# A transformer block's down projection in 2x2 blocks with seven products for eight, in two groups of inner rows

## The chip, the cores and the metric

The kernel runs on one core of a Trainium2 chip. A core has a matrix engine (PE, with a separate row PEld for loading the stationary operand), a vector engine (DVE), a scalar engine (ACT), a general engine (POOL), a sync engine (SP) that here only issues transfers, and 16 DMA engines. Each engine runs its own instructions in order; waits between engines go through semaphores. The metric is the device time of one execution in microseconds (us); the figure for a kernel is the median of its runs.

## The reference

One block of a transformer on `x` of shape (2, 1024, 1024): modulated layer norm, attention with 32 heads, a residual, a second modulated layer norm and a gated feed-forward network whose weights are -1, 0 or +1. What the change touches is the last line of the network:

```python
gate = jnp.einsum('bsh,ih->bsi', x, Wg) * ag
up = jnp.einsum('bsh,ih->bsi', x, Wu) * au
h = jax.nn.silu(gate) * up
out = jnp.einsum('bsi,hi->bsh', h, Wd) * ad      # "down": INTER = 2752 inner rows, 1024 columns
...
x = x + gb * ffn(h2)
```

`gb * ad` is one row vector for each batch, made early and kept in DRAM as `gate_dram[5]`.

## The kernel before

All of it is float32. A product is made from `float32r` operands: the activations are split into a rounded part `hi` and a rest `lo = a - hi`, and both go through PE, while the ternary weights are exact. Counts (`ternary`, `exact`) check on the way that the weights are ternary and the split is exact; if a count is off, `general_block` computes everything again at the end. It doesn't run with these inputs.

The program has an attention stage (until about 1335 us), the output projection and the preparation of the second norm, gate and up for batch 0 and batch 1 (`gate_up`), and down. A list scheduler puts the instructions of each engine in an order. Matmuls are kept in program order in batch 1 of `gate_up` and in down (`pinned`).

Gate and up already use seven products for eight (`SEVEN`, lines 768 to 772): a block product of 2x2 blocks is made as seven products of sums of blocks. Bank `x` or `y` collects a product, some products are kept (`part`) and added to later ones (`MATE`), and four of them finish a quadrant (`QUAD`). `gate_up(b)` runs over eleven pairs `p` of inner blocks (10 of 2x128 rows, the last of 2x96). For each pair:

- `stage(p)` loads four weight tiles of 512 KB on SP's queue into two buffers, one for each half `kh` of the inner dimension. The pool `wst` has two buffers in all.
- `weight_operands` makes seven operands from them: `A11`, `A12`, `A22` are casts on ACT (lines 1611, 1612, 1617), and `S1`, `S2`, `S3`, `S4` are sums on POOL (lines 1613 to 1616). `S3` is the last reader of half 0.
- In batch 1 (and once at the end of batch 0) a tile `wdst` of 1 MB of the down weights goes through the same two buffers: it takes the buffer that `S3` has freed, is loaded on SP (line 1640), counted by DVE (`ternary`, lines 1570 and 1573) and written out to `wd_dram` on SP (line 1642). Half 1 of the next `stage` takes the buffer after it.
- PE runs 7 x 2 x 8 matmuls (gate and up). ACT copies the kept products out of the banks (line 1661), DVE adds, ACT applies silu, DVE multiplies, and SP writes the quadrant to `act_dram` (line 1684).

Down, before: eight token blocks of 128 rows in each of two batches. For each, ACT loads the block of `act_dram` (2816 values a partition) and casts it to `hi` (line 1722), DVE makes `lo` (line 1723), and PE runs 22 inner blocks x 2 halves of the columns x 2 parts = 88 matmuls of 128x512 into two banks (`dn`). DVE multiplies each bank by `gb` (line 1742), POOL adds the residual `x1` (line 1743), and SP writes the output. All of the down weights (11 MB) stand in SBUF, in buffers that `gate_up`'s token tiles leave one after another; their loads start while the last pair still runs.

Of the kernel before, what the change touches and what calls it, by code (L numbers as in the profile page):

```python
# [12 lines left out]
FP = mybir.dt.float32  # L13
FR = mybir.dt.float32r
# [5 lines left out]
P = 128  # L20
# [460 lines left out]
def kernel(  # L481
# [19 lines left out]
    nc = tc.nc  # L501
# [60 lines left out]


    hop2_dram = [dram.tile([P, 7, KC // 2, NJ, P], FP, tag=f"hs_{b}", name=f"hs_{b}") for b in range(B)]
    wd_dram = [dram.tile([P, 2, D], FP, tag=f"wd_{p}", name=f"wd_{p}") for p in range(NPR)]
    act_dram = [dram.tile([P, NJ, 2, NIC, P], FP, tag=f"act_{b}", name=f"act_{b}") for b in range(B)]

    ident = const.tile([P, P], FP, name="ident")
# [1017 lines left out]
    if True:  # L1586
# [6 lines left out]
            return ffp[i // 4].tile([P, 512], FP, tag=f"ff{i}", name=nm)  # L1593

        jkp = ff.enter_context(tc.tile_pool(name="junk", bufs=1))

        with gu:
            W_ORDER = ("A11", "A12", "S2", "S1", "S3", "S4", "A22")
# [27 lines left out]
            def gate_up(b):  # L1626
# [5 lines left out]
                for p in range(NPR):  # L1632
# [4 lines left out]
                    for p_ in down_checks[b].get(p, ()):  # L1637
                        r0, n = PAIRS[p_]
                        t = stp.tile([P, 2, D], FP, tag="wst", name=f"wdst_{p_}")
                        nc.sync.dma_start(t[0:n], wd_t[ds(r0, 2 * n), :].rearrange("(m p) e -> p m e", p=n))  # L1640
                        ternary(t[0:n].rearrange("p m e -> p (m e)"), 2 * NPR + p_, jkp)
                        nc.sync.dma_start(wd_dram[p_][0:n], t[0:n])
                    n = PAIRS[p][1]
                    if p + 1 < NPR or b + 1 < B:
                        st.append(stage((p + 1) % NPR))
# [2 lines left out]
                    for e, (c_, qa, qb_, q) in enumerate(SEVEN):  # L1648
                        done = {}
                        for i, mat in enumerate("gu"):  # L1650
                            ps = bank[mat, c_]
                            for k in range(KC // 2):
                                for hl in range(2):
                                    matmul(
                                        ps[0:n], W[qa][:, i, k, 0:n], tiles[e][:, hl, k, :],
                                        start=(q in ("P1", "P2", "P5") and k == 0 and hl == 0),
                                        stop=(k == KC // 2 - 1 and hl == 1), skip_group_check=True,
                                    )
                            if q in ("P1", "U2", "P5"):
                                part[mat, q] = ptp.tile([P, 512], FP, tag=f"{mat}{q}", name=f"{mat}{q}_{b}_{p}")  # L1660
                                nc.scalar.copy(part[mat, q][0:n], ps[0:n])
                            elif q == "U6":
                                done[mat] = ps
                            else:
                                t = part[mat, MATE[q]]
                                last_read[0] = nc.vector.tensor_add(t[0:n], t[0:n], ps[0:n])  # L1666
                                done[mat] = t
                        if q in QUAD:
                            m, h = QUAD[q]
                            ib = 2 * p + m  # L1670
                            g, u = done["g"], done["u"]
                            if q == "U6":
                                g, u = (
                                    ptp.tile([P, 512], FP, tag=f"{mat}{q}", name=f"{mat}{q}_{b}_{p}") for mat in "gu"
                                )
                            nc.scalar.activation(
                                g[0:n], done["g"][0:n], AF.Silu, scale=vt[0:n, R_AG + ib : R_AG + ib + 1]
                            )
                            ins = nc.vector.scalar_tensor_tensor(
                                u[0:n], done["u"][0:n], vt[0:n, R_AU + ib : R_AU + ib + 1], g[0:n], ALU.mult, ALU.mult  # L1680
                            )
                            if q == "U6":
                                last_read[0] = ins
                            nc.sync.dma_start(
                                act_dram[b][0:n, :, h, ib, :], u[0:n].rearrange("p (j t) -> p j t", j=NJ)
                            )
            for b in range(B):
                pinned[0] = b > 0
                gate_up(b)
            pinned[0] = True  # L1690

        with ExitStack() as dn:
            aip = [own(dn, f"ain{i}") for i in range(2)]
            lop0, hip0, hip1, lop1, gbp = (own(dn, n) for n in ("alo0", "ahi0", "ahi1", "alo1", "gb"))
            wdp = [own(dn, f"wd{p}") for p in range(NPR)]
            xp1, yp = own(dn, "x1in", 2), own(dn, "yout", 2)
            hip, lop = (hip0, hip1), (lop0, lop1)
            dlp = jkp
            wd = [wdp[p].tile([P, 2, D], FR, tag=f"wd{p}", name=f"wd_{p}") for p in range(NPR)]
            gb = []  # L1700

            def more_wd(which):
                for p in which:
                    n = PAIRS[p][1]
                    (nc.scalar if 0 < p < 8 else nc.sync).dma_start(wd[p][0:n].bitcast(FP), wd_dram[p][0:n])

            n1 = PAIRS[-1][1]
            for b in range(B):
                for j in range(NJ):
                    for h in range(2):  # L1710
                        t = 2 * j + h
                        a = aip[h].tile([P, NIC, P], FP, tag=f"ain{h}", name=f"a_{b}_{t}")
                        nc.scalar.dma_start(a[:, 0:WHOLE], act_dram[b][:, j, h, 0:WHOLE])
                        nc.scalar.dma_start(a[0:n1, WHOLE:NIC], act_dram[b][0:n1, j, h, WHOLE:NIC])
                        hi = hip[h].tile([P, NIC, P], FR, tag="ahi", name=f"hi_{b}_{t}")
                        lo = lop[h].tile([P, NIC, P], FR, tag="alo", name=f"lo_{b}_{t}")
                        cuts = [0, 4, 10, WHOLE] if (b, t) == (0, 0) else [0, WHOLE]
                        for v in (
                            *((slice(0, P), slice(u, w)) for u, w in zip(cuts, cuts[1:])),
                            (slice(0, n1), slice(WHOLE, NIC)),  # L1720
                        ):
                            nc.scalar.copy(hi[v[0], v[1]], a[v[0], v[1]])  # L1722
                            nc.vector.tensor_sub(lo[v[0], v[1]], a[v[0], v[1]], hi[v[0], v[1]].bitcast(FP))  # L1723
                        if (b, t) == (0, 0):
                            more_wd(range(NPR))
                            for b_ in range(B):
                                gb.append(gbp.tile([P, D], FP, name=f"gb{b_}"))
                                nc.scalar.dma_start(gb[b_], gate_dram[5][b_].partition_broadcast(P))
                        pss = [ffbank(f"dn_{b}_{t}_{n}") for n in range(2)]
                        for ib in range(NIC):  # L1730
                            rows = PAIRS[ib // 2][1]
                            for s_, src_ in enumerate((hi, lo)):
                                for n in range(2):
                                    matmul(
                                        pss[n], src_[0:rows, ib, :], wd[ib // 2][0:rows, ib % 2, ts(n, HALF)],
                                        start=(ib == 0 and s_ == 0), stop=(ib == NIC - 1 and s_ == 1),
                                    )
                        x1 = xp1.tile([P, D], FP, tag="x1", name=f"x1_{b}_{t}")
                        nc.sync.dma_start(x1, x1_dram[b * NT + t])
                        y = yp.tile([P, D], FP, tag="y", name=f"y_{b}_{t}")  # L1740
                        for n in range(2):
                            nc.vector.tensor_mul(y[:, ts(n, HALF)], pss[n], gb[b][:, ts(n, HALF)])  # L1742
                            nc.gpsimd.tensor_add(y[:, ts(n, HALF)], y[:, ts(n, HALF)], x1[:, ts(n, HALF)])  # L1743
                            nc.sync.dma_start(out[b, ts(t, P), ts(n, HALF)], y[:, ts(n, HALF)])
                        if (b, t) == (0, 0):
                            for i, src_ in enumerate((hi, lo)):
                                exact(
                                    src_[:, 0:4].rearrange("p k t -> p (k t)"), NCOUNT + i, ffbank(f"probe{2 + i}"), dlp
                                )
                        if (b, t) == (1, 2):  # L1750
                            verdict(dlp, ffbank)


    ff.close()
# [50 lines left out]
```

## Time and profile before

| | us |
|---|---|
| median of three runs (2352.24 to 2357.76) | 2355.83 |
| the profiled execution's own time | 2356.1 |
| its span on the core | 2354.4 |
| batch 0 to batch 1 of `gate_up` at PE | 1721 |
| first matmul of down | 2019.4 |
| last matmul of down starts | 2345.5 |

Busy time by engine and the main stages' shares, from the page's first part and from a table by stretches of time (columns: the stretch, then busy us and instructions of PE, PEld, DVE, ACT and POOL, then PE's granted clock, the DMA engines' busy share, GB/s):

```profile
PE 2198.6 (93%) x9713; PEld 1211.6 (51%) x9713; DVE 1266.9 (54%) x1820; ACT 841.8 (36%) x1701; POOL 886.8 (38%) x679
1800.00:2000.00 200.00, 196.71 (x861) 160.29 (x861) 103.25 (x106) 70.19 (x102) 76.92 (x32) 1.00 0.60 191
2100.00:2200.00 100.00, 100.00 (x442) 82.61 (x441) 27.62 (x20) 13.23 (x10) 12.69 (x10) 1.00 0.35 124
```

A busy share near 1 on PE in the last two lines says that matmuls follow each other almost without a gap there. The engines beside it are busy for about half of batch 1's gate and up and for about a fifth of down.

### The profile page before, as it was taken

Reading aid. Unit: us, or ns where it says so; the run is one execution under the profiler, and the core shown is the slowest. Engines: PE = TensorE matmul, PEld = TensorE weight load, DVE = VectorE, ACT = ScalarE, POOL = GpSimd, SP = SyncE. Lnnn points to the kernel's source line nnn. Section 1 sums busy time; section 2 is a strip of 40 time slices with the busy share of each in tenths; the row PEclk is TensorE's granted clock in tenths of the full one; section 3 lists DMA queues with packets and bytes.
Section 4 is the critical chain, followed back from the end, with each engine's and each line's share of the span. In section 5 each row is a group of like instructions: output and inputs, shape, how many; then the busy total and the mean of one; then the engine's idle time right before and its main releaser. Section 6 shows DMA issues by size and latency. Waiting matters only on the chain.

```text
span 2354.4 us, 26878 instructions
## 1 busy us (share of the span) xinstructions
PE 2198.6 (93%) x9713; PEld 1211.6 (51%) x9713; DVE 1266.9 (54%) x1820; ACT 841.8 (36%) x1701; POOL 886.8 (38%) x679
## 2 busy tenths in 40 slices
PE   6999999999999998798888797999989999999998
PEld 2444443333333332232222245888767788788887
DVE  5775752456556343366765566667785454322221
ACT  1322224444444445465555224333343333211110
POOL 2330202442336455666575653344343342011111
PEclk9999999999999999999999998999999999999999
DMA  9887777346246323754532466433476656833331
GB/s 368 307 305 274 287 269 242 133 135 221 94 155 217 134 90 141 209 166 130 153 117 90 127 201 219 128 114 117 131 267 214 201 182 198 334 126 126 124 104 38
DMA packets 264034, 423.18 MB, mean 180 GB/s; under 512 B 12940, under 2 KB 198604, under 8 KB 250132
## 3 DMA queue, kind: packets, MB, share of 16 engines
q1 hardware_dynamic: 256048, 382.00, 48.7%
q10 hardware_dynamic: 7844, 39.37, 4.6%
q8 instruction: 79, 1.29, 0.2%
q14 instruction: 63, 0.52, 0.1%
HBM read 290.51 MB, written 130.81 MB: 179 GB/s over the span
## 4 chain that ended last, share of the span: by engine, by line
PE 30%; DVE 7%; issue 7%; DMA 4%; POOL 3%; ACT 1%; SPq 0%; DVEq 0%; POOLq 0%; ACTq 0%
PE dn L742 12%; PE ux L742 4%; PE gx L742 4%; PE uy L742 4%; PE gy L742 3%; PE bank L742 2%; DVE junk L1570 2%; DVE p L1106 1%; DMA wst<-in_L_ffn_Wu_dram 1%; DMA wd<-wd 1%; DVE junk L1573 1%; PE sc L742 1%; DMA traw<-hs 1%; ACT p L1074 1%; PE av L742 1%
## 5 line engine op out<-in xcount | busy, mean ns | idle before, releaser
L1074 ACT ACTIVATE p<-sc,kw 128x128 f32<-128x128 f32 (+3 forms) x1024 | 422.6, 514 | 394.7 <-PE sc L742 374.9
L742 PE MATMUL bank<-wT,a 128*128 128x512 f32 x768 | 365.8, 610 | 14.5 <-ACT P L966 8.0
L1106 POOL TENSOR_TENSOR p<-p,p 128x1024 f32<-128x1024 f32 (+3 forms) x128 | 263.6, 2060 | 238.9 <-PE av L742 209.2
L1106 DVE TENSOR_TENSOR p<-p,p 128x1024 f32<-128x1024 f32 (+3 forms) x192 | 235.9, 1243 | 141.7 <-POOL p L1078 75.5
L742 PE MATMUL bank<-wB,a 128*128 128x512 f32 x576 | 270.3, 605 | 1.9 <-DVE raw L973 1.4
L742 PEld LDWEIGHTS bank<-wT,a 128*128 128x128 f32 x768 | 136.7, 191 | 199.0 <-issue 166.5
L742 PE MATMUL dn<-wd,hi 128*128 128x512 f32 (+1 forms) x704 | 218.4, 391 | 2.5 <-DMA wd<-wd 2.5
L742 PE MATMUL sc<-cq,ck 32*128 32x512 f32 (+3 forms) x1536 | 185.2, 543 | 37.5 <-ACT p L1074 28.7
L742 PE MATMUL dn<-wd,lo 128*128 128x512 f32 (+1 forms) x704 | 218.0, 391 | 1.0 <-DVE lo L1723 1.0
L1078 POOL TENSOR_SCALAR_AFFINE_SELECT p<-p 128x256 f32<-128x256 f32 x256 | 130.5, 522 | 187.0 <-ACT p L1074 177.5
L742 PE MATMUL av<-p,cv 128*32 128x512 f32 (+3 forms) x1536 | 169.9, 507 | 13.9 <-POOL p L1078 13.9
L742 PEld LDWEIGHTS bank<-wB,a 128*128 128x128 f32 x576 | 102.1, 189 | 145.8 <-issue 125.1
L1613 POOL TENSOR_TENSOR wS<-wst,wst 128x1024 fp32r<-128x1024 f32 (+1 forms) x22 | 53.5, 2430 | 304.2 <-DMA wst<-in_L_ffn_Wu_dram 213.9
L1743 POOL TENSOR_TENSOR y<-y,x 128x512 f32<-128x512 f32 x32 | 40.8, 1293 | 316.1 <-DVE y L1742 316.1
L742 PEld LDWEIGHTS dn<-wd,hi 128*128 128x128 f32 (+1 forms) x704 | 132.6, 189 | 30.9 <-DMA wd<-wd 3.0
L742 PEld LDWEIGHTS sc<-cq,ck 32*128 32x128 f32 x1536 | 62.8, 185 | 166.0 <-issue 97.9
L742 PEld LDWEIGHTS dn<-wd,lo 128*128 128x128 f32 (+1 forms) x704 | 132.6, 188 | 29.7 <-DVE lo L1723 1.5
L1742 DVE TENSOR_TENSOR y<-dn,gb 128x512 f32<-128x512 f32 x32 | 20.6, 686 | 209.0 <-issue 196.6
L1722 ACT CAST hi<-a 96x256 fp32r<-96x256 f32 (+4 forms) x34 | 42.5, 1300 | 247.3 <-PE dn L742 223.4
L742 PEld LDWEIGHTS av<-p,cv 128*32 128x32 f32 x1536 | 32.5, 109 | 140.7 <-issue 78.3
L742 PE MATMUL gy<-hs,wS 128*128 128x512 f32 (+1 forms) x352 | 91.4, 402 | 7.8 <-DVE gP L1666 5.3
L742 PE MATMUL uy<-hs,wS 128*128 128x512 f32 (+1 forms) x352 | 91.0, 401 | 6.4 <-DVE uP L1666 6.4
(224 smaller groups left out, 3298.0 us busy)
## 6 DMA issues: line engine op xcount, KB each, us to landing
a<-hop SPq DMA_DIRECT2D x20, 1792.0 KB
wm<-in_L_wmod_dram SPq DMA_DIRECT2D x48, 512.0 KB
wB<-in_L_attn_Wqkv_dram SPq DMA_DIRECT2D x21, 1024.0 KB
wst<-in_L_ffn_Wg_dram SPq DMA_DIRECT2D x40, 512.0 KB
wst<-in_L_ffn_Wu_dram SPq DMA_DIRECT2D x40, 512.0 KB
a<-act ACTq DMA_DIRECT2D x16, 1280.0 KB
qk<-qs SPq DMA_DIRECT2D x16, 1024.0 KB
hop<-a SPq DMA_DIRECT2D x8, 1792.0 KB
```

What stands on the lines that cost most here:

```text
L742: return in_order(nc.tensor.matmul(*args, **kw_))
L1074: last_exp[0] = nc.scalar.activation(p[:, g, lo:hi], sp[:, g, lo:hi], AF.Exp, bias=kw[:, d, h_ : h_ + 1])
L1078: last_mask[0] = nc.gpsimd.affine_select(out=p[:, :, 0:P], in_=p[:, :, 0:P], pattern=[[0, 2], [1, P]], compare_op=ALU.is_ge, fill=0.0, bas ...
L1106: adders[b](half, jb).tensor_add(dst, dst, ps[half][:, :, 0:n])
L1570: hold(nc.vector.scalar_tensor_tensor(j, w, 0.0, w, ALU.is_gt, ALU.not_equal, accum_out=count_a[0:n, at : at + 1]))
L1573: hold(nc.vector.tensor_scalar(j, w, -1.0, None, ALU.is_equal, ALU.add, accum_out=count_b[0:n, at : at + 1]))
L1613: nc.gpsimd.tensor_add(f["S1"], raw["A21"], raw["A22"])
L1722: nc.scalar.copy(hi[v[0], v[1]], a[v[0], v[1]])
L1742: nc.vector.tensor_mul(y[:, ts(n, HALF)], pss[n], gb[b][:, ts(n, HALF)])
L1743: nc.gpsimd.tensor_add(y[:, ts(n, HALF)], y[:, ts(n, HALF)], x1[:, ts(n, HALF)])
```

## The change

Down is computed like gate and up, with seven products for eight. The four blocks of the left side are two token blocks of 128 rows by two halves of a pair of inner blocks; those of the right side are two inner halves by two halves of the columns. One product then handles 256 tokens, so there are four blocks `j` for each batch. The right side needs seven operands: three blocks of `Wd` as they are and four sums.

- The seven operands of all eleven pairs don't fit in SBUF at once, so down runs twice over all tokens, first over pairs 0 to 5 and then over pairs 6 to 10 (`g` = 0, 1). The first pass adds its part, times `gb`, to `x1` and writes it back to `x1_dram`; the second reads it from there and writes the output.
- The four sums are made on POOL in `gate_up`, where `wdst` passes through, and seven operands of 256 KB for each pair are written to `wdt_dram` in place of the 1 MB to `wd_dram`.
- The left side needs four sums in each block of tokens: `S1`, `S2` on DVE, `S3`, `S4` on POOL. Each of the seven left operands is split into `hi` and `lo`, in groups (`a1` for `A11` and `A12`, `s12`, `s34`, `a22`).
- The rows above 96 of the last pair are filled with zeros.

```diff
-    wd_dram = [dram.tile([P, 2, D], FP, tag=f"wd_{p}", name=f"wd_{p}") for p in range(NPR)]
+    SPLIT = ((0, (NPR + 1) // 2), ((NPR + 1) // 2, NPR))
+    DC = SPLIT[0][1]
+    wdt_dram = [dram.tile([P, 7, DC, HALF], FP, tag=f"wdt_{g}", name=f"wdt_{g}") for g in range(2)]
...
                         ternary(t[0:n].rearrange("p m e -> p (m e)"), 2 * NPR + p_, jkp)
-                        nc.sync.dma_start(wd_dram[p_][0:n], t[0:n])
+                        if n < P:
+                            nc.gpsimd.memset(t[n:P], 0.0)
+                        b11, b12, b21, b22 = (t[:, kh, ts(h, HALF)] for kh in range(2) for h in range(2))
+                        v = wtp.tile([P, 4, HALF], FP, tag="wdsum", name=f"wdsum_{p_}")
+                        nc.gpsimd.tensor_sub(v[:, 0], b12, b11)
+                        nc.gpsimd.tensor_sub(v[:, 1], b22, v[:, 0])
+                        nc.gpsimd.tensor_sub(v[:, 2], b22, b12)
+                        nc.gpsimd.tensor_sub(v[:, 3], b21, v[:, 1])
+                        dst = wdt_dram[p_ // DC][:, :, p_ % DC]
+                        nc.sync.dma_start(dst[:, 0], b11)
+                        nc.sync.dma_start(dst[:, 1:3], t[:, 1].rearrange("p (h e) -> p h e", h=2))
+                        nc.sync.dma_start(dst[:, 3:7], v)
...
+            raw0 = slot("raw0", [P, 2, 2 * DC, P])
+            a22p = slot("a22", [P, 2, DC, P], FR)
+            parts = {"P1": slot("dP1", [P, HALF])}
+            s12p = slot("s12", [P, 2, 2, DC, P], FR)
+            a1p = slot("a1", [P, 2, 2 * DC, P], FR)
+            s34p = slot("s34", [P, 2, 2, DC, P], FR)
...
+            accp = slot("acc", [P, 2, D], FP, 2)
...
+            def token_parts(g, b, j):
...
+                nc.scalar.dma_start(r[:, :, 0 : 2 * n], act_dram[b][:, j, :, ds(2 * c0, 2 * n)])
...
+                def two(dst, src, eng):
+                    nc.scalar.copy(dst[:, 0], src)
+                    eng.tensor_sub(dst[:, 1], src, dst[:, 0].bitcast(FP))
+
+                two(a1[:, :, 0 : 2 * n], r[:, 0, 0 : 2 * n], nc.vector)
+                nc.vector.tensor_add(s[:, 1], a["A21"], a["A22"])
+                nc.vector.tensor_sub(s[:, 0], s[:, 1], a["A11"])
+                nc.gpsimd.tensor_sub(s[:, 2], a["A11"], a["A21"])
+                nc.gpsimd.tensor_sub(s[:, 3], a["A12"], s[:, 0])
+                two(s12[:, :, :, 0:n], s[:, 0:2], nc.vector)
+                two(s34[:, :, :, 0:n], s[:, 2:4], nc.vector)
+                two(a22[:, :, 0:n], a["A22"], nc.gpsimd)
...
+            for g in range(2):
...
+                    eng = nc.scalar if g == 0 and 0 < e < 5 else nc.sync
+                    eng.dma_start(wd[q][:, 0:n].bitcast(FP), wdt_dram[g][:, W_SLOT[q], 0:n])
+                for b in range(B):
+                    for j in range(NJ):
...
+                            nc.sync.dma_start(acc[:, m], x1_dram[b * NT + 2 * j + m])
+                        bank = {c_: ffbank(f"d{c_}_{at}") for c_ in "xy"}
+                        part = {}
+                        for c_, qa, qb_, q in SEVEN:
+                            for k_ in range(n):
+                                for l in range(2):
                                     matmul(
+                                        bank[c_], left[qa](l, k_), wd[qb_][:, k_],
...
+                            if q in ("P1", "U2", "P5"):
+                                part[q] = parts[q](at)
+                                nc.scalar.copy(part[q], bank[c_])
+                                continue
+                            m, h = QUAD[q]
+                            y = part[MATE.get(q, "P5")]
+                            if q == "U6":
+                                nc.vector.tensor_mul(y, gb[b][:, ts(h, HALF)], bank[c_])
+                            else:
+                                nc.vector.tensor_add(y, y, bank[c_])
+                                nc.vector.tensor_mul(y, y, gb[b][:, ts(h, HALF)])
+                            nc.gpsimd.tensor_add(acc[:, m, ts(h, HALF)], acc[:, m, ts(h, HALF)], y)
+                            if g == 1:
+                                nc.sync.dma_start(out[b, ds((2 * j + m) * P, P), ts(h, HALF)], acc[:, m, ts(h, HALF)])
+                        if g == 0:
+                            for m in range(2):
+                                nc.sync.dma_start(x1_dram[b * NT + 2 * j + m], acc[:, m])
```

The order in which the changed program's instructions stand on each engine, as far as the prediction speaks of it:

- SP, for each pair of batch 1 from the third on: the first quadrant to `act_dram`, the load of `wdst`, two quadrants, two `wdt` transfers (blocks as they are), the last quadrant, the `wdt` transfer of the four sums, then the four `wst` loads of the next pair. Before, `wdst`'s 1 MB went out where the two `wdt` transfers stand, and the `wst` loads followed the last quadrant.
- ACT, in the same pairs: after the copy of U2's gate comes the cast `A11` of the next pair, then the copies of U2's up and P5's gate, then the cast `A12`, then the copy of P5's up.
- In down, from the third block on, for block k. ACT: the cast of `a22` for k, the load of the raw block k+2, the copy of P1, the cast of `a1` for k+1, the copies of U2 and P5, the casts of `s12` and `s34` for k+1. DVE: P2's add and multiply, `lo` of `a1` and of `s12` for k+1, U3's add and multiply, P53's add and multiply, `lo` of `s34` for k+1, U6's multiply, `S1` and `S2` for k+2. POOL: P2's, U3's and P53's residual adds, `S3` for k+2, `lo` of `a22` for k+1, U6's residual add, `S4` for k+2.

## The prediction

> **What bounds the kernel now.** I read the table by stretches first (PE is busy all the time in both stages that change), then the chain of waits to the end, then the timelines of single engines. The chain (start, us, what):
>
> ```profile
> 2036.09 9.19 PE dn L742 x32
> ...
> 2045.75 200.01 PE dn L742 x880
> ...
> 2245.87 66.20 PE dn L742 x292
> ```
>
> Down is PE and nothing else: 200.01 / 880 = 0.2273 us a matmul. Beside it DVE and POOL have room, but not at the same time. Two pairs of timeline rows (start, us, engine, line):
>
> ```profile
> 1721.39 5.60 POOL L1614 TENSOR_TENSOR wS<-wS,wst 128x1024 fp32r<-128x1024 f32 x1
> 1722.45 2.27 DVE L1570 SCALAR_TENSOR_TENSOR junk<-wst 128x2048 bf16<-128x2048 f32 x1
> ```
>
> ```profile
> 2126.39 2.54 POOL L1743 TENSOR_TENSOR y<-y,x 128x512 f32<-128x512 f32 x2 [17.46 <-DVE y L1742]
> 2127.71 3.90 DVE L1723 TENSOR_TENSOR lo<-a,hi 128x2560 fp32r<-128x2560 f32 x1 [0.80 <-ACT hi L1722]
> ```
>
> POOL's 128x1024 sum is 2.40 us elsewhere; here it ends at 1726.99, 2.27 after DVE's operation ended (1724.72). `lo` of 2560 is 2.82 at 2043.04; here it ends at 2131.61, 2.68 after POOL's (2128.93). An operation with two SBUF inputs on one of the two engines waits for the other's to end, then takes its time less 0.14. With one input in PSUM it doesn't wait (0.68 to 0.69 throughout).
>
> In batch 1's gate and up the weights come in a loop. One turn (POOL, SP and ACT rows):
>
> ```profile
> 1854.46 2.41 POOL L1613 TENSOR_TENSOR wS<-wst,wst 128x1024 fp32r<-128x1024 f32 x1 [15.46 <-PE uy L742]
> ...
> 1880.13 2.40 POOL L1613 TENSOR_TENSOR wS<-wst,wst 128x1024 fp32r<-128x1024 f32 x1 [15.62 <-DMA wst<-in_L_ffn_Wu_dram]
> ```
>
> ```profile
> 1861.73 0.37 SPq L1640 DMA_DIRECT2D wdst<-in_L_ffn_Wd_dram  x1
> ...
> 1867.01 0.34 SPq L1642 DMA_DIRECT2D wd<-wdst  x1
> 1867.40 0.52 SPq L1684 DMA_DIRECT2D act<-uU  x1
> 1868.08 1.30 SPq L1514 DMA_DIRECT2D wst<-in_L_ffn_Wg_dram  x1
> ...
> 1871.67 0.37 SPq L1514 DMA_DIRECT2D wst<-in_L_ffn_Wg_dram  x1
> ```
>
> ```profile
> 1880.03 1.05 ACT L1612 CAST wA<-wst 128x1024 fp32r<-128x1024 f32 x1 [1.31 <-DMA wst<-in_L_ffn_Wu_dram]
> 1880.98 0.57 ACT L1661 COPY uU<-ux 128x512 f32<-128x512 f32 x1
> ```
>
> The turn: sums from 1854.46, `S3` done and `wdst` issued 1861.73 (+7.3; 7.7 in other turns), landed 1867.01 (+5.3), counted on DVE until 1871.6, then half 1 of the next `wst`, landed 1880.03. It takes 25.7; PE's pair takes 7 x 16 x 0.2273 = 25.4. The loop is at its bound already, and a late cast on ACT holds the copy behind it, which PE waits for:
>
> ```profile
> PE ux L742 <- ACT uU L1661: 3.1, 3, 1.5
> ```
>
> From pair 1's first product (1757.8) to pair 10's (1993.6) it is 235.8 for 9 x 25.4 = 228.6: 7.2 lost.
>
> **The change, part 1: matmuls.** Before 16 x 88 = 1408; after 2 batches x 4 blocks x 7 products x 2 parts x 11 = 1232. 176 fewer x 0.2273 = 40.0 us less on the path, if PE stays the bound. A block of tokens is 84 matmuls = 19.1 us in group 0 and 70 = 15.9 in group 1.
>
> **Part 2: weight sums in batch 1.** POOL gets 4 sums of 128x512 for each pair (1.27 each, half of the 2.54 above). POOL is idle for 15 us of a turn, so its time is free; its place isn't. The sums start when `wdst` lands, together with DVE's count of two SBUF inputs (2.29): 2.29 + 4 x 1.27 - 0.14 = 7.2 until the last. Behind them on SP stands the transfer of the sums, and behind that all four `wst` loads, which before left 1 us after landing. So at landing + 7.4 SP issues 1 MB of sums and 2 MB of `wst`. 1 MB alone took 5.3 (`wdst`); 2 more MB at the 0.35 MB/us of this stage's full microseconds (333 to 365 GB/s from 1872 to 1878) are 5.7: landed at +18.4, before +13.0. The turn becomes 7.7 + 5.3 + 18.4 = 31.4, and 6.0 us a pair go to PE: ACT's casts `A11` and `A12` wait for `wst`, behind them stand the copies of U2's and P5's up halves, and PE's U3 and P53 wait for these. The first such pair still has room (half 0 lands 17.3 after the pair's start, cast and copy end at 18.9, PE needs it at 16.3: 2.6). Sum: 8 x 6.0 + 2.6 - 2 (the last pair's loads are 3/4) - 7.2 (lost before already) + 4 (change of batch, where the same sums stand ahead of the token loads and DVE is full; estimated from the 8.0 us that PE waits there now, bounds 0 and 8) = +45. Bounds of the turn: 28.6 (no lock, 0.40 MB/us, the fullest slices) to 33.7 (`wdst` 6.8 as at 1809.98, rate 0.31 as over whole 13 us of transfers), so +16 to +70.
>
> In sentences of its own: the Trainium skill's page "DMA: Bandwidth & Descriptors", section Bandwidth, gives 425 GB/s for very long transfers from HBM. This case's full microseconds in this stage show about 350; by the page's rate the 2 MB would take 4.7, the turn 30.4, and the sum would be 8 us lower.
>
> **Part 3: a block of down, hand-scheduled.** Operations of two SBUF inputs for a wide block: DVE 2 sums of 768 (0.95 by the 768 row), 3 `lo` of 1536 (1.75, between 1.48 for 1280 and 2.28 for 2048), 3 multiplies (0.68); POOL 3 of 768 (1.85) and 4 adds of 512 (1.27). Together 19.8 us, 17.7 when each follows another (less 15 x 0.14), beside 19.1 of PE. They needn't exceed PE to hurt: they queue in order. From block k's start (T = 0): the last two of the block before, `lo` of `s34` and P53's add, hold the port until 2.0. Then by turns DVE `S1` to 2.8, POOL `S3` to 4.5, DVE `S2` to 5.4, POOL `lo` of `a22` to 7.1. Only now is the raw buffer free, which ACT waits for in its load (0.35), and behind the load stands the copy of P1 (0.59): 8.0. U2 adds to P1's bank, and PE came to it at 5.4. PE waits 2.6. Later `lo` of `s12`, U3's add and multiply, and `lo` of `s34` run late by the same, and the next block starts as this one: period 21.6. In group 1 the same gives 18.9 to 19.0. Before, the same share of the work took 21.8 and 18.2 (6/11 and 5/11 of 176 x 0.2273). So the seven-for-eight gain is paid back: 8 x 21.6 + 8 x 19.0 = 324.8 against 320. Lower bound, no lock: PE's pace, 280.
>
> Again apart: "SBUF — State Buffer", section Who interferes with whom, says that the first of the two engines keeps the shared port for its whole instruction. The rows give 0.14 less; by the page the wide block needs 19.8 of port, more than PE, and the waits grow by about 1 us a block, +16.
>
> **Part 4: start and end of down.** E is the end of gate and up (2019.5 now). Before, the first matmul came at E because its buffers were free. `a1` lies on the buffers of `S3`, `S4` and `A22`, which PE reads last: cast 1.5 and `lo` 1.75 stand open, +3.3. In block 0 DVE's U3 add stands behind the sums of block 1. Now the second token load lands at 2040.67 (E + 21); new ones ahead of it are `acc` (2 MB) and `gb` (0.5) less 0.5 MB of weights: 2 / 0.36 (the mean of 1997 to 2045) = 5.6, less 2.3 for an earlier issue, E + 24; two sums, cast, `lo`, add are 5.9, so U6 starts at E + 30, block 0 ends at E + 32.7. In block 1 ACT's cast of `a1` stands behind `a22`'s, which waits for block 0's end; with DVE's probes ahead of `lo`, 7 us open: block 1 ends at E + 60. Then 6 x 21.6 + 8 x 19.0 = 281.6, reloading the weights between the groups +3 (8.75 MB plus 5 of others at 0.36 in some 35 us; bounds 0 and 8), the last block without a next one -2: E + 342.6. The last add is one quarter, not two: 8.5 - 1.3 = 7.2 to the end of the span. E + 349.8 against 334.9 now: +15. Bounds: -28 without the lock (6 x 2.5 + 8 x 3.1 for the blocks, 4 at the start), +30 with the upper ends.
>
> **Sum.** 2354.4 + 45 + 15 = 2414.4 span; 1.7 lie outside it (2356.1 - 2354.4): 2416. The profiled run is 0.3 above the median of three.
>
> **Rivals.**
> - A: down runs at PE's pace although the loop is slow (POOL and DVE fall into a rhythm that hides the waits): 2354.4 + 45 - 25 + 1.7 = 2376. For: 17.7 of port under 19.1 of PE. Against: the ACT load that waits for POOL's last `a22`.
> - B: the loop costs nothing beyond the change of batch, +4, because operands are made up to 10.9 us before their pair starts: 2354.4 + 4 + 15 + 1.7 = 2375. Against: the copies behind the casts leave about 1 us of that, and PE waits there already.
> - C, the other side: POOL and DVE don't exclude each other in these shapes. The sums then end 2.2 earlier and `S3` 0.45: turn 28.7, 3.3 a pair, 8 x 3.3 - 2 - 7.2 + 4 = +21, of which 1 goes as the first pairs have room; down -28: 2354.4 + 20 - 28 + 1.7 = 2348. It decides from a turn of about 29.5 with blocks at PE's pace. Against: both pairs of rows above.
> - That it doesn't remove matmuls is excluded: the built order holds 1232.
>
> **Numbers.** Forecast 0.64, A 0.12, B 0.12, C 0.08, later than the range 0.04. 0.2% is 4.7 us, about what the runs before spread (5.5). Faster: C and a tail, 0.09; within 0.2%: 0.02; slower: 0.89. The forecast's own range is 2372 to 2446 (part 2 at +16 with down at 0, part 2 at +60 with down at +30); with A and B it is 2370 to 2446.
>
> **What would show it.** Between the first sums (`S1`) of successive pairs in batch 1: 31, not 25.5, PE waiting for ACT's copies of U2 and P5. In down: blocks of 21 to 22 and 19, PE's waits on ACT at U2, POOL and DVE rows stretched by each other. A gap of 10 us or more in block 0. I am wrong if `wst` lands within 15 us of `wdst`, or if PE has no gap at U2.

## The result, and the profile after

The changed kernel takes 2462.9 us, the median of four runs (2458.9 to 2470.3), beside 2356.6 for the kernel before in the same runs (2352.2 to 2357.8): ratio 1.0458, 95% interval 1.0430 to 1.0487. The forecast was 2416, so the sign was right and the size was not: 106 us more where 60 were expected, and outside the range.

The profiled execution took 2463.96, span 2462.2. Cut at the first matmul of gate and up and at the first of down, the two spans compare so:

| stage | before | after | difference | forecast |
|---|---|---|---|---|
| up to gate and up (no edit touches it) | 1408.8 | 1413.3 | +4.5 | 0 |
| gate and up | 610.5 | 673.6 | +63.1 | +45 |
| down, to the span's end | 335.0 | 375.3 | +40.3 | +15 |

The 4.5 is within the spread: over the fourteen executions profiled here the first matmul of gate and up lies anywhere from 1406.8 to 1418.6. So the experiments below are read by the two stages, which don't hold it.

**One turn of batch 1's loop**, in the changed kernel's timeline (start, us, engine, line, tiles; in brackets the idle time before and what ended it), first POOL, then SP:

```profile
1825.56 2.37 POOL L1616 TENSOR_TENSOR wS<-wst,wst 128x1024 fp32r<-128x1024 f32 x1 [11.59 <-DMA wst<-in_L_ffn_Wu_dram]
...
1839.20 3.40 POOL L1649 TENSOR_TENSOR wdsum<-wdst 128x512 f32<-128x512 f32 x1 [3.28 <-DMA wdst<-in_L_ffn_Wd_dram]
...
1845.19 1.29 POOL L1652 TENSOR_TENSOR wdsum<-wdst,wdsum 128x512 f32<-128x512 f32 x1
1858.11 2.39 POOL L1616 TENSOR_TENSOR wS<-wst,wst 128x1024 fp32r<-128x1024 f32 x1 [11.63 <-DMA wst<-in_L_ffn_Wu_dram]
```

```profile
1833.58 0.37 SPq L1643 DMA_DIRECT2D wdst<-in_L_ffn_Wd_dram  x1
...
1846.51 0.36 SPq L1656 DMA_DIRECT2D wdt<-wdsum  x1
1846.96 0.46 SPq L1516 DMA_DIRECT2D wst<-in_L_ffn_Wg_dram  x1
```

From `S1` to `S1` it is 32.55. `wdst` goes out at +8.0, lands 5.6 later, the four sums are over 7.3 after that, and all four `wst` loads stand behind the megabyte of sums on SP; `S1` follows 18.9 after `wdst` landed. From pair 3 on, PE's waits (total, times, longest) are the ones named in the forecast, for copies that stand behind the late casts on ACT; in pair 2 it waits 5.2 for DVE and 3.2 for another copy:

```profile
PE ux L744 <- ACT uU L1675: 33.9, 7, 6.5
```

**A steady block of down**: PE, then the end of POOL's work for the block and ACT's:

```profile
2186.74 4.62 PE L744 MATMUL dx<-wdT,s 128*128 128x512 f32 x12 [2.44 <-ACT dP L1787]
2191.19 2.88 PE L744 MATMUL dy<-wdT,s 128*128 128x512 f32 x12
...
2210.11 2.50 PE L744 MATMUL dx<-wdT,s 128*128 128x512 f32 x7 [2.44 <-ACT dP L1787]
```

```profile
2201.25 2.78 POOL L1796 TENSOR_TENSOR acc<-acc,dU 128x512 f32<-128x512 f32 x1 [0.63 <-DVE dU L1795]
2203.99 2.56 POOL L1745 TENSOR_TENSOR dsum<-raw 128x768 f32<-128x768 f32 x1
2206.51 2.52 POOL L1740 TENSOR_TENSOR a<-raw,a 128x768 fp32r<-128x768 f32 x1
```

```profile
2209.07 0.37 ACTq L1730 DMA_DIRECT2D raw<-act  x1
2209.47 0.58 ACT L1787 COPY dP<-dx 128x512 f32<-128x512 f32 x1 [6.36 <-POOL a L1740]
```

POOL's last `lo` ends at 2209.03, ACT's load of the raw buffer goes out at once, the copy of P1 follows, and U2 starts 2.44 late. So far it is the forecast. What it had not: U2's twelve matmuls, which take 2.72 from start to start in the next product, take 4.45 here. The table by stretches gives the reason (stretch, length, busy time and instructions of PE, PEld, DVE, ACT, POOL, then PE's granted clock, share and GB/s of the transfers):

```profile
2183.00:2184.00 1.00, 1.00 (x6) 0.75 (x4) 0.99 (x1) 0.00 (x0) 1.00 (x2) 1.00 0.00 0
2186.70:2188.00 1.30, 1.26 (x4) 1.03 (x5) 1.25 (x2) 1.30 (x1) 1.30 (x2) 0.71 0.90 213
2188.00:2189.00 1.00, 1.00 (x3) 0.78 (x3) 1.00 (x1) 0.06 (x1) 0.69 (x1) 0.50 1.12 424
2189.00:2190.00 1.00, 1.00 (x4) 0.74 (x3) 1.00 (x2) 0.00 (x0) 0.69 (x1) 0.50 0.98 270
2190.00:2191.20 1.20, 1.20 (x6) 0.96 (x5) 0.90 (x1) 0.00 (x0) 1.20 (x1) 0.72 0.91 247
2191.20:2194.00 2.80, 2.80 (x14) 2.33 (x13) 0.00 (x0) 0.59 (x1) 0.85 (x1) 1.00 0.72 296
```

The granted clock is 1.00 ahead of the gap, 0.50 from soon after it, and 1.00 again from 2191. Over the whole of down:

```profile
2086.60:2454.00 367.40, 308.48 (x1235) 246.73 (x1235) 229.78 (x201) 102.40 (x112) 212.39 (x109) 0.92 0.52 189
```

1232 matmuls and two probes at 0.2267 are 279.8; PE is busy for 308.5, so 28.7 us are slow matmuls. Its waits add up to 58.9. 279.8 + 28.7 + 58.9 and 7.9 of tail are the 375.3.

### The profile page after: what moved, and what is told of

Its sections match the earlier page's. It is cut to its first block, busy times and chain, and to the rows that moved or that the text cites. A ratio compares the mean times of both kernels' runs of the same rounds, so it can differ in the third digit from the quotient of the medians.

```text
span 2462.2 us, 27072 instructions
## 1 busy us (share of the span) xinstructions
PE 2211.4 (90%) x9537; PEld 1208.3 (49%) x9537; DVE 1424.1 (58%) x1946; ACT 900.2 (37%) x1779; POOL 1156.5 (47%) x812
## 4 chain that ended last, share of the span: by engine, by line
PE 17%; POOL 12%; DMA 9%; DVE 8%; issue 6%; ACT 2%; SPq 1%; ACTq 0%; POOLq 0%; DVEq 0%
DMA wst<-in_L_ffn_Wu_dram 3%; PE dx L744 3%; DMA wdst<-in_L_ffn_Wd_dram 2%; PE gx L744 2%; PE ux L744 2%; PE dy L744 2%; PE bank L744 2%; PE uy L744 2%; POOL acc L1796 2%; DVE junk L1572 2%; PE gy L744 2%; DVE p L1108 1%; POOL wdsum L1649 1%; POOL a L1740 1%; POOL dsum L1745 1%
## 5 line engine op out<-in xcount | busy, mean ns | idle before, releaser
L744 PE MATMUL dx<-wdT,s 128*128 128x512 f32 x352 | 101.9, 445 | 39.9 <-ACT dP L1787 38.6
L1796 POOL TENSOR_TENSOR acc<-acc,dP 128x512 f32<-128x512 f32 x48 | 82.4, 1717 | 104.3 <-DVE dP L1795 102.6
L744 PE MATMUL ux<-hs,wS 128*128 128x512 f32 (+1 forms) x352 | 98.0, 424 | 33.9 <-ACT uU L1675 33.9
L744 PEld LDWEIGHTS dx<-wdT,s 128*128 128x128 f32 x352 | 75.4, 218 | 62.5 <-ACT dP L1787 45.8
L744 PEld LDWEIGHTS av<-p,cv 128*32 128x32 f32 x1536 | 32.3, 108 | 140.4 <-issue 80.2
L744 PE MATMUL gx<-hs,wS 128*128 128x512 f32 (+1 forms) x352 | 92.3, 405 | 8.9 <-POOL wS L1617 5.3
L744 PEld LDWEIGHTS ux<-hs,wS 128*128 128x128 f32 (+1 forms) x352 | 71.1, 204 | 53.3 <-ACT uU L1675 36.9
L1740 DVE TENSOR_TENSOR s<-dsum,s 128x1536 fp32r<-128x1536 f32 (+1 forms) x32 | 54.1, 1691 | 70.8 <-ACT s L1739 70.8
```

The costliest lines, as they stand in the source:

```text
L744: return in_order(nc.tensor.matmul(*args, **kw_))
L1740: eng.tensor_sub(dst[:, 1], src, dst[:, 0].bitcast(FP))
L1796: nc.gpsimd.tensor_add(acc[:, m, ts(h, HALF)], acc[:, m, ts(h, HALF)], y)
```

## The experiments

Each changes the changed kernel unless it says otherwise. The time is one run's, except for e12. "Gate/up" and "down" are the stages of the table above, taken from each profiled execution. Where an edit doesn't touch a stage, it repeats within some 4 us (gate/up in e3 and e4, down in e1, e2 and e5).

| run | time | before beside it | gate/up | down |
|---|---|---|---|---|
| e1_sums_last | 2417.9 | 2358.0 | 629.9 | 379.4 |
| e2_wdst_own | 2437.5 | 2358.0 | 641.8 | 375.4 |
| e3_raw_on_sp | 2426.0 | 2358.0 | 673.6 | 338.6 |
| e4_pe_kept_busy | 2459.7 | 2358.0 | 676.8 | 367.5 |
| e5_wd_spread | 2409.5 | 2356.4 | 616.7 | 374.4 |
| e6_both | 2368.7 | 2356.4 | 614.3 | 340.6 |
| e7_start_of_down | 2355.5 | 2356.4 | 619.1 | 321.1 |
| e8_before_own | 2352.0 | 2356.4 | 603.4 | 336.1 |
| e9_start_2 | 2348.3 | 2359.9 | 627.2 | 309.4 |
| e10_start_3 | 2341.4 | 2359.9 | 615.3 | 313.7 |
| e11_pairs_of_wd | 2356.1 | 2359.9 | 632.5 | 313.2 |
| e12_best (median of 6) | 2348.7 | 2358.7 | 619.0 | 315.6 |

### The loop of batch 1: e1 and e2

```diff
-                        nc.sync.dma_start(dst[:, 3:7], v)
+                        late = (dst[:, 3:7], v)
...
                         st.append(stage((p + 1) % NPR))
+                    if late:
+                        in_order(nc.sync.dma_start(*late))
```

> The changed kernel, but in batch 1 the transfer of the weight sums stands behind the wst loads of the next pair on SP instead of ahead of them, with those transfers kept in written order. My theory (half 1 of the next wst, and half 0 with it, go out only after the four sums and their 1 MB transfer): half 0 goes out at wdst's landing, half 1 right after the sums without a megabyte ahead of it, and lands about 13 us after wdst instead of 18.9; the turn from S1 to S1 falls from 32.3 to about 27, PE's waits for uU's copies nearly go, end of gate and up about 45 us earlier, about 2418 in all. Rival (the four sums themselves, or the extra megabytes, set the turn): the turn stays above 31 and the time within 10 of 2463.

Measured: 2417.9, gate/up 43.7 shorter. SP and PE's waits in pairs 1 to 10:

```profile
1856.98 0.34 SPq L1655 DMA_DIRECT2D wdt<-wdst  x1
...
1857.90 0.45 SPq L1516 DMA_DIRECT2D wst<-in_L_ffn_Wg_dram  x1
...
1864.66 0.37 SPq L1516 DMA_DIRECT2D wst<-in_L_ffn_Wg_dram  x1
...
1865.62 0.51 SPq L1662 DMA_DIRECT2D wdt<-wdsum  x1
```

```profile
PE uy L744 <- DVE uP L1683: 13.2, 8, 2.0
```

Half 0 goes out 0.9 after `wdst` landed, half 1 right after the sums, and the turn is 27.8 (`S1` at 1843.35 and 1871.15), 27.4 in the mean. The sums themselves, their megabyte and the lock are all still there, so it was the place on the queue.

```diff
-                        t = stp.tile([P, 2, D], FP, tag="wst", name=f"wdst_{p_}")
+                        if p_ < 2:
+                            t = stp.tile([P, 2, D], FP, tag="wst", name=f"wdst_{p_}")
+                        else:
+                            t = right["raw"][p_ % 2].tile([P, KC // 2, NJ * P], FP, tag=f"traw{p_ % 2}", name=f"wdst_{p_}")
```

> The changed kernel, but from the third wdst on it lies in the two buffers that the token loads leave free after the change of batch, and its load stands behind the wst loads of the next pair: the weights of gate and up no longer wait for counts or sums. My theory (the loop through the shared wst buffer is what costs): turns of 25.4 to 25.6, PE's own pace, no waits of PE on uU's copies after pair 2; end of gate and up about 50 us earlier, total about 2412. Rival (volume of transfers, or DVE and POOL holding each other up, makes the stage slow): turns stay above 29 and the gain is under 25.

Measured: 2437.5, half a miss. In the loop PE is left with waits of at most 1.2, but the later turns are 26.5 to 29 (27.5 in the mean), not 25.4 to 25.6. And the change of batch got longer: PE waits 15.9 there for `A11`, 11.0 of it at the start of pair 1. A buffer of its own brings the loop no further than e1's order on the queue does with the shared one, so the order is most of what the loop cost; the change of batch is a cost of its own, which e5 takes away.

### Down: e3 and e4

```diff
-                nc.scalar.dma_start(r[:, :, 0 : 2 * n], act_dram[b][:, j, :, ds(2 * c0, 2 * n)])
+                nc.sync.dma_start(r[:, :, 0 : 2 * n], act_dram[b][:, j, :, ds(2 * c0, 2 * n)])
```

> The changed kernel, but down's token load (raw) is issued by SP, not by ACT, so that the copy of P1 doesn't stand behind a load that waits for POOL's lo of a22. My theory (the order on ACT makes the wait at U2): the 2.44 and 3.09 us at U2 go, with them the slow products after them (4.6 for 2.7), blocks of 19.1 to 20 in group 0 and 16 to 17.5 in group 1, total 45 to 62 lower: 2401 to 2418. Rival (the operations of DVE and POOL that exclude each other set the period whatever ACT does): blocks stay at 21 or more and 19 or more, the waits move to U3 or U6, gain under 25.

Measured: 2426.0; gate/up as it was, down 36.7 shorter. PE, ACT and SP in a steady block:

```profile
2172.43 2.88 PE L744 MATMUL dy<-wdB,a 128*128 128x512 f32 x12
2175.15 2.88 PE L744 MATMUL dx<-wdT,s 128*128 128x512 f32 x12
```

```profile
2172.68 0.59 ACT L1787 COPY dP<-dx 128x512 f32<-128x512 f32 x1 [1.88 <-PE dx L744]
```

```profile
2176.78 0.37 SPq L1730 DMA_DIRECT2D raw<-act  x1
```

The load still waits for POOL and goes out at 2176.78; the copy of P1, 4 us earlier, waits for PE alone. Blocks take 19.04 and 15.9 to 16.2, PE's own pace, with DVE busy for 15.5 and POOL for 15.4 of 19 us (14.9 and 14.8 in a block of the changed kernel). DVE and POOL hold each other up as much as before; in the steady blocks it costs nothing once no copy stands behind them. The rival falls. The gain is 37 and not the 45 to 62 expected, as there are new waits for the weights and for DVE at the change of groups (7.0, 5.0 and 4.0).

```diff
                         for c_, qa, qb_, q in SEVEN:
+                            if q == "U2":
+                                idle = ffbank(f"idle_{at}")
+                                for i in range(11):
+                                    matmul(idle, left["S1"](0, 0), wd["T1"][:, 0], start=True, stop=True)
```

> The changed kernel with 11 more matmuls in each block of down, between P2 and U2, into a bank that nobody reads (2.50 us of work where PE waited 2.44 to 3.09). Theory (PE's clock is lowered for some 3.3 us after a gap, so each gap costs 1.7 to 1.9 us on top of itself): with the gap filled the twelve matmuls of U2 take 2.73 again, blocks of 21.5 and about 19.1, total about 20 lower, 2443, although there are 176 more matmuls. Rival (U2's matmuls are slow because DVE, POOL and the transfers work on the same memory just then): U2 still takes 4.6 and the time stays or rises by up to 5.

Measured: 2459.7; the profile has 7.8 less in down, not 20. The mechanism is as the theory has it:

```profile
2188.72 2.65 PE L744 MATMUL idle<-wdT,s 128*128 128x512 f32 x11
2191.35 3.01 PE L744 MATMUL dx<-wdT,s 128*128 128x512 f32 x12
2194.20 2.88 PE L744 MATMUL dy<-wdT,s 128*128 128x512 f32 x12
```

```profile
2163.00:2278.00 115.00, 115.00 (x504) 94.01 (x504) 80.70 (x63) 35.11 (x37) 79.81 (x40) 1.00 0.48 163
```

With the gap filled by work the clock stays at 1.00, U2 takes 2.85, and a block with eleven matmuls more takes 21.8 where it took 23.3 (19.3 for 20.9 in group 1). The size was wrong: the nine blocks that had a slow U2 behind this wait are 13.2 shorter together and the first of group 1 is 2.5 shorter, but the other six, where the filler stands in no gap, in a short one or in one of another cause, are 8.3 longer.

### Both stages mended: e5 to e8

e5 puts the load of `wdst` and the three transfers behind `stage(...)`, all in the token buffers, and moves two of them:

```diff
-            down_checks = ({NPR - 1: [0]}, {p: [p + 1] for p in range(NPR - 1)})
+            down_checks = ({4: [0], 7: [1]}, {p: [p + 1] for p in range(1, NPR - 1)})
```

> The changed kernel with all wdst loads in the two buffers of the token loads, behind the wst loads of the next pair, and the first two of them moved out of the change of batch into pairs 4 and 7 of batch 0. Theory (the shared wst buffer makes the loop, the change of batch costs because counts, sums and token loads meet there): PE waits at the change of batch no more than before (8 us in all), pairs of 26.5 to 27 in batch 1, end of gate and up near 2029 instead of 2086.6, total about 2406. Rival (DVE is too full in batch 0, or POOL's sums hold it up): the pairs 4 and 7 of batch 0 get longer by over 3 us each and the total stays above 2430.

> e5_wd_spread and down's token load on SP (e3_raw_on_sp) together. Theory: the two costs lie in different stages and add: 57 + 37 below the changed kernel, about 2369. Rival: with gate and up faster, the weights of down come too late and down gives back over 15.

Measured: 2409.5 and 2368.7. e5 takes 56.9 of the 63.1 out of gate and up, e6 adds 33.8 in down: the two causes lie in different stages and add. What stays: after pairs 4 and 7 of batch 0 PE waits at P5, 3.7 and 4.1 in e7's profile, with slow matmuls after it. That part of e5's rival came true: the two pairs behind are 5 longer each (31.0 and 31.4 for 26.0), though the total is far below its 2430.

e8 is the same for the kernel before, whose loop was at its bound too:

> The kernel before with the edits of e5_wd_spread (its wd passes in the token buffers, two of them in batch 0; down unchanged). Theory (its loop was at its bound and lost about 7 us in batch 1 and up to 8 at the change of batch): 8 to 15 lower, about 2346. Rival (there is nothing to win, the loop hid behind PE): within 3 of before.

Measured: 2352.0, gate/up 7.1 shorter. One run each, so 4 us of total are no more than a hint; the pairs are the better witness: the one at the change of batch takes 30.5 for 36.9, pairs 1 to 9 of batch 1 together 5.3 less, pairs 5 and 8 of batch 0 together 6.6 more.

e7 lays out down's buffers anew, moves the probes and the order of loads:

```diff
+                            if q == "U2" and (g, b, j) == (0, 0, 0):
+                                for i in range(2):
+                                    exact(a1[:, i, 0:4].rearrange("p k t -> p (k t)"), NCOUNT + i, ffbank(f"probe{i}"), jkp)
...
                         left, a1 = token_parts(g, b, j)
+                        if k + 1 < len(blocks):
+                            load_tokens(*blocks[k + 1])
```

> e6_both and three edits to the start of down: buffers laid so that a1 and dsum lie where gate and up is done early and s34 not on tiles that an act transfer still reads; the probes of a1 right after the second product of block 0; the token load of the next block ahead of gb and acc on SP. Theory (block 0 waits for act<-uU's transfer through s34, block 1 for the probes that hold a1): the 7.5 us at U2 of block 0, the 10.3 us at a1 of block 1 and the slow products after them go, total about 24 below e6, 2345. Rival (the first blocks wait for the weights' transfers, 10 MB at 0.36 MB/us): PE waits on wd in block 0 instead, gain under 8.

Measured: 2355.5, 13 of the 24. Block 1 has no wait any more: the probes had held `a1`. Block 0 still waits 9.5 at U2, since my layout had missed its aim (`s34` still lay where a transfer of gate and up reads); the ACT row of e7:

```profile
2048.65 1.47 ACT L1753 CAST s<-dsum 128x1536 fp32r<-128x1536 f32 x1 [14.82 <-DMA act<-uU]
```

### Where the transfers set the pace: e9 to e12

e9 moves `s34`, loads the second token block ahead of the weights, and puts two stores behind the reload of the weights. e10 puts that token load behind the weights again, e11 has no `wdst` in batch 0 and two in pairs 2 and 5 of batch 1, e12 is e10 with ACT's casts for block 1 behind the copy of P5 of block 0.

> e7_start_of_down with s34 off every tile that an act transfer reads (in e7 it still lay on three of them), the second token load of down ahead of the weights on SP, and the last two x1 stores of group 0 behind the reload of the weights on SP instead of ahead of four of them. Theory (the remaining waits of PE are orders on queues, not the rate of the transfers): the 9.5 us at U2 of block 0 and the 1.6 and 1.5 after it go, the 7.5 at P5 of the first block of group 1 goes, with the slow products after them: 18 to 25 below e7, 2331 to 2338. Rival (at the start of down and between the groups the transfers run at their full rate, 0.41 to 0.43 MB/us, and PE waits for weights wherever the queue puts them): the waits come back as PE waits on wd, gain under 8.

> e9_start_2, but the second token load of down goes out behind the weights again (in e9 PE waited 6.5 us for the first weights behind it). Theory (from E - 20 to E + 20 the transfers run at 0.42 MB/us, so only their order can be chosen, and this one brings each before PE needs it except the second token load, some 4 us late): P1 of block 0 starts within 2 us of E, PE waits under 3 us in block 0 and 3 to 5 at block 1; 4 to 9 below e9, 2339 to 2344. Rival (any order loses the same): within 3 of e9.

> e10_start_3 with no wdst in batch 0: all eleven in pairs 1 to 9 of batch 1, two of them in pairs 2 and 5. Theory (in pairs 4 and 7 of batch 0 six counts on DVE and the sums meet, and PE waits there 4.4 + 1.5 us with a lowered clock after it; batch 1 has no counts of wst): these two stalls of some 6 go and pairs 2 and 5 of batch 1 lose at most 2 each: 6 to 10 below e10. Rival (POOL's 19.7 us of sums in a pair of 25.4, with the counts between, stop PE there): no gain or a loss up to 6.

> e10_start_3 with ACT's casts for block 1 held behind the copy of P5 of block 0 (in e10 the cast of a1, which waits for the second token load, stood ahead of that copy and PE waited 7.3 us at P53). Theory: that wait and the slow products after it go (9.3), and half of it comes back at U6, where DVE's add stands behind the sums of block 1: 3 to 5 below e10, 2336 to 2339, against before 0.990 to 0.994. Rival (the second token load decides, whatever stands behind it): within 1.5 of e10.

e9, 7 below e7 (with the kernel before 3.4 higher beside it), is a draw: between the groups the theory holds (7.5 and 0.4 of waits for weights became four of 0.57 or less), at the start the rival does. PE in e9, and two stretches:

```profile
2037.23 5.00 PE L744 MATMUL dx<-wdB,a 128*128 128x512 f32 x12 [6.47 <-DMA wdB<-wdt]
```

```profile
2030.00:2035.00 5.00, 0.76 (x4) 0.23 (x2) 4.15 (x3) 1.79 (x2) 4.52 (x2) 0.97 1.01 430
2035.00:2040.00 5.00, 2.77 (x7) 2.23 (x8) 3.42 (x3) 2.16 (x2) 2.40 (x2) 0.50 1.02 430
```

Every transfer engine is busy, at 430 GB/s, and PE waits for the first weights behind 1.5 MB of tokens.

e10 took 2341.4, as expected, but by luck: gate and up's end no longer waits, and PE waits 12.1 in block 0, not under 3. 7.3 of them are at P53, for a copy behind the cast of `a1` for block 1. The token load lands 3.0 ahead of that cast; what ends its wait is DVE's probe of the old `a1`, which stands behind a multiply that waited 9.5 for `gb`. e11 fell to its rival: after pair 2 of batch 1 PE waits 1.5 for DVE and 6.3 for a copy, after pair 5 it waits 3.2 and 6.5, and gate and up is 17 longer than in e10. e12 is a miss too: the wait at P53 went, and the whole of it came back at U6, where DVE's add stands behind a multiply that waited for `gb` and the sums of block 1 that follow it (DVE, then PE):

```profile
2057.06 1.11 DVE L1827 TENSOR_TENSOR dP<-dP,gb 128x512 f32<-128x512 f32 x1 [10.91 <-DMA gb<-gate]
...
2065.69 4.99 PE L744 MATMUL dx<-wdT,a 128*128 128x512 f32 x12 [10.82 <-DVE dP L1826]
```

In both, `gb`, which stands behind the second token load on SP, lands some 1.2 after it; no run with this order puts `gb` ahead.

e12's six runs against eleven of the kernel before give a ratio of 0.9944, interval 0.9925 to 0.9963: with its queues in order the changed kernel is 10 us faster than the kernel before, not 106 slower. Part of that is e5's edits, which help the kernel before as well (e8, 4 us in one run), so how much the seven products themselves bring, some 6 us or less, is not shown.

## Why the prediction was wrong

**Matmuls (part 1).** Right in count and in price at full clock: 1232 at 0.2267.

**Waits in down (parts 3 and 4).** Right in size. Taking the forecast's 349.8 for down, less 7.2 of tail and 280 of matmuls, leaves 62.6 of waits; 58.9 came: 22.6 in the first two blocks (21.8 said), 13.7 in the other six of group 0 (15.0), 22.7 in group 1 (25.8). The last is partly luck: the change of groups took 5.2 for 3, and the last two blocks, where ACT has no load left to issue, wait for nothing. U2's wait was put at 2.6 and is 2.44 in four of the six steady blocks (1.9 and 2.0 in the others), for the reason given: the DVE and POOL rows stretch each other (2.78, 2.56, 2.52 for 1.27, 1.85, 1.85) and ACT's load stands ahead of the copy. Within the sum two causes at the start were wrong. `a1` was said to lie on the buffers of `S3`, `S4` and `A22`; in the built kernel it lies on those of `A11`, `A12` and `S2`, and P1 is 2.1 late (3.3 was said) because the cast stands behind an activation on ACT. And block 0 waits 7.5 at U2 for a transfer, not for DVE (the ACT row of the changed kernel):

```profile
2099.44 1.47 ACT L1739 CAST s<-dsum 128x1536 fp32r<-128x1536 f32 x1 [11.25 <-DMA act<-uU]
```

**The step that failed.** Part 3 says "period 21.6" as 19.1 of PE plus 2.6 of wait: every matmul at 0.2273 whatever came ahead of it. With the wait of 2.44 the period is 23.3 to 23.4, and in group 1 20.85 where 19.0 was said. The missing term is the clock: 28.7 us of slow matmuls in down, which the forecast put at nothing (the kernel before has some 3: 322.9 busy for 1410 matmuls). Some 17 of them fall in the steady blocks, 8 in the first two blocks and 4 at the change of groups. Less the 3.7 of waits that didn't come, with 0.7 more of tail, they are the whole miss of down (375.3 for 349.8). Of the 48 us by which the span missed its 2414.4, that is 25.5; gate and up makes 18, and 4.5 stand ahead of both. e3 takes the gaps away and the periods fall to PE's pace; e4 leaves the order and fills the gaps, and the slow matmuls go. The profile before had shown it at the change of batch, eight matmuls whose row is 2.0 long elsewhere:

```profile
1736.42 3.62 PE L742 MATMUL gy<-hs,wS 128*128 128x512 f32 x8 [4.42 <-DVE gP L1666]
```

I had read the 4.42 and not the 3.62.

**The loop (part 2).** The mechanism is right, and e1 shows its place; the term was undersized. The turn was put at 31.4 and is 32.3 from pair 4 on, in its three parts 7.7, 5.7 and 18.9 for 7.7, 5.3 and 18.4. From P1 of pair 1 to P1 of pair 10 the loop costs 54.4 more than before, for 41.4: against 25.4 a pair, pairs 1 and 2 lose 12.0 for 8.6, pairs 3 to 9 49.7 for 40, of which the longer turn makes some 6; the rest is not taken apart. From the last sum to `S1` it is 11.6 for the 11.2 assumed; whether the megabyte of sums or the size of its pieces makes the 0.4 was not tried. Of the 61.7 that these pairs take above PE's pace 42.5 are waits and 19 slow matmuls; where the turn sets the pace, slow matmuls fill time in which PE would have waited (argued, not tried).

**The change of batch.** +4 was said, and the pair at it went from 36.9 to 45.4. Two things: waits of 14.2 for 8.0, and more slow matmuls. At one of the waits POOL and DVE don't take turns, as the forecast had them do in part 3 (POOL, then DVE):

```profile
1731.46 7.75 POOL L1617 TENSOR_TENSOR wS<-wS,wst 128x1024 fp32r<-128x1024 f32 x1
```

```profile
1732.51 2.27 DVE L1572 SCALAR_TENSOR_TENSOR junk<-wst 128x2048 bf16<-128x2048 f32 x1
...
1734.72 2.28 DVE L1531 TENSOR_TENSOR hs<-traw,hs 128x2048 fp32r<-128x2048 f32 x1
1736.92 2.27 DVE L1575 TENSOR_SCALAR_CACHE_REDUCE junk<-wst 128x2048 bf16<-128x2048 f32 x1
```

POOL's sum, 2.4 by itself, was held through two operations of DVE in a row, not through one: the first two of these rows, each with two inputs in SBUF. It ends at 1739.21, 2.21 after the second of them, as the forecast's rule on the lock has it; the third, with one input, ran beside it. PE waited 5.3 for the sum.

**The rivals.** A, down at PE's pace, gave the right price for the way things could be (e3: 19.04) and was rightly held unlikely, because of ACT's load. B fell. C fell by the stretched rows; but its view that the lock need not cost anything in down holds in the steady blocks as soon as no copy waits behind it. What came, a time beyond the range, had been given 0.04. Of the signs named, the late `wst` and the waits for copies came; the blocks took 23 and 21 us, not 21 to 22 and 19, and the longest gap in block 0 is 7.5, not 10.

## What to carry to other kernels

Price a gap of PE at more than its length: here one of 2.4 us mostly costs 1.7 more and one of 7.5 us 1.6 more, so many short gaps are dearer than one long one, and a wait that is a tenth of a block can eat a saving of an eighth. On an engine that issues transfers as well as working, look for a load that waits for another engine ahead of a copy that PE waits for; moving the issue to another queue was worth 37 us. Where a staging buffer is shared, what is made from it is better written out behind the loads of the next turn (44 us in e1).

## What the runs showed of the hardware that was not expected

- After a gap of 2.44 us PE's granted clock falls to 0.50 and is back at 1.00 some 3.4 us later (by the means of the stretches shown: from 2187.25 to 2190.67). While PE works in the changed kernel's down, each lowered stretch is 3.41 us long, or two or four times that, whatever the gap; 3.41 us at half the clock are 1.7 us lost, the price found above. Gaps of 1.9 to 2.0 us cost only 0.1 more in the changed kernel (two of the six steady periods of group 0), but not always: in e1 one of 1.91 was followed by twelve matmuls of 4.54, and one of 2.44 by twelve of 3.02. The Trainium skill, "TensorE: Matmul & The Clock Gate", section "Part 1: The HAM clock gate", tells of a half-rate clock after an idle window of some 3.4 us that runs free, and of full rate after such a window of work. Half rate and the 3.4 us of return agree with the rows; a gap well below 3.4 us was enough here.
- An operation of POOL that waits for DVE can be passed over once more when DVE has another of two SBUF inputs ready (7.75 us for 2.4). One of DVE with a single input ran beside it, neither longer for it (2.27 us).
- From 2015 to 2040 in e9 the transfers run at 413 to 430 GB/s; the forecast's 0.36 MB/us for the start of down was low. In the loop of the changed kernel the stretches of 2 us from 1848 to 1858, ahead of `S1`, moved 236 to 374, though the transfer engines are as busy. The figure of the Trainium skill, "DMA: Bandwidth & Descriptors", section Bandwidth (425 GB/s for 16 MB), fits the first and not the second.
